# A perceiver layer on one core: pools of their own for keys and ctx weights, the last projection ahead of the experts' blocks, experts' matrices asked for one by one, deeper buffers in the late scan

## The chip, the cores and the metric

The kernel runs on one core of one Trainium2 chip. The metric is the device time of one execution in microseconds (us); lower is better. The kernel before took 1546.52 us in the median of three runs (1540.41 to 1550.73). All data are fp32.

The names of the engines in the profile: PE is TensorE (matmuls; PEld is its loading of weights), DVE is VectorE, ACT is ScalarE, POOL is GpSimd, SP is SyncE, which here only issues transfers (DMAs). Each engine works through its own list of instructions in order; an instruction that has to wait holds everything behind it on its engine.

## The reference, cut to what matters

Four batches of 256 tokens of width 256 go through one layer of three parts, each added to the residual stream x:

```python
x = x + cross_attention(layernorm(x), ctx)      # 8 heads of 64; keys and values of
                                                # 256 own + 4096 ctx positions
# mixture of depths: a small router sorts each batch's tokens
xn      = layernorm(x)
s       = gelu(xn @ r_w1 + r_b1) @ r_w2
top 64 tokens of a batch    -> self-attention of 16 heads
the other 192, in order     -> ssm: conv, silu, h = dA * h + dBu, y = sum(h * C), gate
x = x + scattered back
# mixture of experts, 8 experts, 2 per token
top_w, top_i = top_k(softmax(x @ router_w.T), 2)
h = silu(x @ gate[e]) * (x @ up[e]);  y = h @ down[e]
x = x + sum over the two experts of top_w * y
```

## The kernel before, in words

**The attention's loop** (L1205 to 1634) has 128 steps n, each one eighth of a group G of two heads of one batch, and two more to run out. A step makes scores (L1374), takes the maximum and the exponentials, turns them on DVE (`pt`, L1438) and multiplies them with the values (`po`, L1447). In between it makes the next group's keys (`k_chunk` L1321, `k_self`) and values (`v_chunk` L1351) from ctx chunks. Weights of the group, the batch's turned input `x1T` and the keys `kt` all come from the pool `wk`, together with the work tiles of scores and exponentials. When the last group of a batch is through, `finish_batch` (L1504) multiplies the heads' outputs with the output weights (`project`, L1492) and adds the product to x (`add`, L1500). For the last batch most of that product stands inside the loop's last step; what is left, the last pair of heads of the second half, is queued as a background task.

**Background tasks.** Other parts of the layer are written as generators: `routed(b)` (L892) is the router, the self-attention of the top tokens, the ssm with its scan, and the way back for batch b; `sortable` and `dispatch` (L1039) choose experts for the tokens of tiles 0 to 5 and sort them into blocks of one expert each. A planner places them in the program: `slot(budget)` (L1168) goes through the list of active tasks and runs a task on by one `yield` if its due time has come and its stated cost fits the budget; `now` is moved on by an estimate of the work in front. So the order of the instructions on every engine is fixed when the program is built; there is no scheduler beside it. Three batches' tasks fit beside the attention. The last batch's (b = 3) need the attention's end and run beside the experts' blocks; they use `ssm_scan_late` (L777).

**The late scan.** 16 steps i. ACT makes the decays `dal` (four exponentials of 128x191, L805) one step ahead into one of two tiles `das`; DVE multiplies (L838), scans (L839), multiplies by C (L845) and adds halves (L846) in a tile `db` of three buffers; PE adds up the rest (`yps`, L813). After the scan the gate (`zs`, L866), two products on PE (`pssd` L871, `psback` L881) and an addition bring the batch back to x; then `prepare` (L1792) makes the input of the dense experts.

**The blocks** (`ordered`, L1680). 19 blocks (NB) of 128 sorted tokens. For each block j: three loads of 512 KB, gateT, upT and downT, of the block's expert, whose number SP reads from a tile (L1686); a gather of 128 rows (`xg`, POOL, L1700); a turn on PE and a copy on ACT (`psxb`, `xTb`, L1712, L1715); `half(j, 0)` and `half(j, 1)`, 16 matmuls each into `p0b` and `p1b` (L1721), which come from one pool of three PSUM tiles; `gated` (L1668): a tanh on ACT, two operations on DVE; and, one block later, `down(j - 1)`: eight matmuls into `pdb` (L1735), a copy on ACT (`yb`, L1742) and the write of 128 rows to memory (`ysd`, L1743). The loads and the write are all issued by SP: blocks 0 to 2 are loaded ahead, and `load(j + 2)` comes at the end of block j, behind the write of block j - 1. The experts' tiles come from the pool `fw` with three buffers for each of the three names; this pool is opened after those of the attention are closed, so its tiles lie where theirs lay, and a first load waits for the last reader there.

**The end.** `collect` (L1769) gathers for each token its two rows of `ysd` and adds them. Tiles 6 and 7 (256 tokens) go through all 8 experts densely (`experts`, L1837): for each expert gate, up and down products. Experts 0 and 1 are loaded by `load(NB)` and `load(NB + 1)` in `ordered`, the next always one ahead.

Of the kernel before, what the change touches and what calls it, by code (L numbers as in the profile page):

```python
# [8 lines left out]
F32 = mybir.dt.float32  # L9
# [5 lines left out]
P = 128  # L15
# [3 lines left out]
KD = D // P  # L19
# [27 lines left out]
def perceiver_layer(ctx: ExitStack, tc: tile.TileContext, a: dict, out: bass.AP):  # L47
# [729 lines left out]
    def ssm_scan_late(b, st):  # L777

        SG = 4
        K = DS // SG
        pool = late["pool"]
        delta = st["delta"]
        spread = {}

        das = [pool.tile([P, SG, NBOT], F32, name=f"dal{i}") for i in range(2)]
        for t in das:
            nc.gpsimd.memset(t[:, :, 0:1], 0.0)

        def load(k):
            if k < K:
                for o, name in enumerate(("bbl", "cbl")):
                    t = spread[k, o] = pool.tile([P, SG, NBOT], F32, tag=name, name=name, bufs=2)
                    nc.scalar.dma_start(
                        out=t,
                        in_=st["bcd"][o, SG * k : SG * (k + 1), :].partition_broadcast(P),
                    )


        def decay(i):
            k, m = divmod(i, NDT)
            if k < K:
                for s in range(SG):
                    nc.scalar.activation(  # L805
                        das[i % 2][:, s, 1:], delta[:, m, 1:], AF.Exp,
                        scale=cs["amat"][:, m, SG * k + s : SG * k + s + 1],
                    )
# [12 lines left out]

        yps = st["yps"] = late["psum"].tile([P, 2, 512], F32, name="yps")
        zero = pool.tile([P, SG, NBOT], F32, tag="dbl", name="zero", bufs=3)[:, :2]
        nc.gpsimd.memset(zero, 0.0)
        for i in range(2):
            nc.tensor.matmul(
                yps[:, i, : 2 * NBOT], ident, zero.rearrange("p s t -> p (s t)"),
                start=True, stop=False,
            )
        yield 0.0, 0  # L830
        decay(0)
        yield 0.0, 3.8
        u = st["u"]
        for i in range(K * NDT):
            k, m = divmod(i, NDT)
            decay(i + 1)
            db = dbl[i] = pool.tile([P, SG, NBOT], F32, tag="dbl", name="db", bufs=3)
            nc.vector.tensor_tensor(db, spread[k, 0], bc(u[:, m, :], 1, SG), ALU.mult)  # L838
            nc.vector.tensor_tensor_scan(  # L839
                out=db.rearrange("p s t -> p (s t)"),  # L840
                data0=das[i % 2].rearrange("p s t -> p (s t)"),
                data1=db.rearrange("p s t -> p (s t)"),
                initial=0.0, op0=ALU.mult, op1=ALU.add,
            )
# [358 lines left out]
    NG = B * NHP  # L1203
    NJ = QK // 32
    with ExitStack() as s1:  # L1205
        ctp = s1.enter_context(tc.tile_pool(name="xctx", bufs=4))
        wk = s1.enter_context(tc.tile_pool(name="xwk", bufs=2))
        ps_s = s1.enter_context(tc.tile_pool(name="ps_s", bufs=1, space=PSUM))

        def load_weights(G, names, tag, bufs):  # L1210
            hp = G % NHP
            t = wk.tile([P, len(names), KD, P], F32, tag=tag, name=tag, bufs=bufs)
            for i, name in enumerate(names):
                nc.sync.dma_start(
                    out=t[:, i],
                    in_=a[name].rearrange("(c p) m -> p c m", p=P)[:, :, hp * P : (hp + 1) * P],
                )
            return t
# [68 lines left out]
            yield  # L1287

        def turn_x(b):
            x1Ts[b] = wk.tile([P, KD, T], F32, tag="x1T", name="x1T", bufs=1)  # L1290
            ps = bank("psx1")
            for c in range(KD):
                for h in range(2):
                    nc.tensor.transpose(
                        ps[:, c * T + h * P : c * T + (h + 1) * P],
                        x1s[b][:, h, c * P : (c + 1) * P], ident,
                    )
            nc.scalar.copy(x1Ts[b].rearrange("p c t -> p (c t)"), ps)
# [22 lines left out]
        def k_chunk(G, g):  # L1321
            b = G // NHP
            if G not in kts:
                kts[G] = wk.tile([P, 4, QK], F32, tag="kt", name="kt")
            ct = load_ctx(b, g)
            ps = ps_m.tile([P, 512], F32, tag="m", name="psk")
            for c in range(KD):
                nc.tensor.matmul(  # L1328
                    ps, wqk[G][:, 0, c, :], ct[:, c, :],
                    start=(c == 0), stop=(c == KD - 1),  # L1330
                )
            keys_out(G, g * (CK // 4), ps)

        def k_self(G):
            x1T = x1Ts[G // NHP]
            if G not in kts:
                kts[G] = wk.tile([P, 4, QK], F32, tag="kt", name="kt")
            ps = ps_m.tile([P, 512], F32, tag="m", name="psks")
            for i in range(2):
                for c in range(KD):  # L1340
# [178 lines left out]
        with tc.manual_schedule():  # L1519
# [14 lines left out]
            for n in range(N + 2):  # L1534
# [61 lines left out]
                else:  # L1596
# [25 lines left out]
                        turn(n - 1, 1)  # L1622
                    if last:
                        normalize(m)
                        if m % 8 == 7:
                            start_first(finish_batch(m // 8))
                b = n // 32 + 1
                if b < B:
# [14 lines left out]
    with ExitStack() as s4, tc.manual_schedule():  # L1643
# [7 lines left out]

        late["pool"] = s4.enter_context(tc.tile_pool(name="late", bufs=1))

        def load_expert(e):
            ts = []
            for name, n, m in (("gateT", KD, HID), ("upT", KD, HID), ("downT", NHC, D)):
                t = fw.tile([P, n, m], F32, tag=name, name=name)
                view = a[name].rearrange("e (c p) m -> p e c m", p=P)
                if isinstance(e, int):
                    nc.sync.dma_start(out=t, in_=view[:, e])  # L1660
                else:
                    nc.sync.dma_start(
                        out=bc(t, 1, 1), in_=view[:, bass.ds(e, 1)]
                    )
                ts.append(t)
            return ts

        def gated(pg, pu, out, n):  # L1668

# [9 lines left out]

        def ordered():  # L1680

            weights = {}

            def load(j):
                if j < NB:
                    e = nc.values_load(  # L1686
                        order["experts"][0:1, j : j + 1], engines=[mybir.EngineType.SP],
                        min_val=0, max_val=E - 1,
                    )
                    weights[j] = load_expert(e)  # L1690
                else:
                    first[j - NB] = load_expert(j - NB)

            ys = dram.tile([NB * P, D], F32, name="ysd", bufs=1)
            xgs, xTs, hs = {}, {}, {}
# [34 lines left out]
            def down(j):  # L1730
# [9 lines left out]
                        yield 0.86  # L1740
                y = fk.tile([P, D], F32, name="yb")
                nc.scalar.copy(y, ps[:, :D])  # L1742
                nc.sync.dma_start(out=ys[j * P : (j + 1) * P, :], in_=y)  # L1743
                yield 0.86

            for j in range(3):
                load(j)
            for j in range(4):
                gather(j)
            turn_block(0)  # L1750
            for j in range(NB):
                pg = yield from half(j, 0)
                pu = yield from half(j, 1)
                turn_block(j + 1)
                gather(j + 4)
                rest = down(j - 1)
                yield next(rest, 0.9)

                hs[j] = fk.tile([P, NHC, P], F32, name="hb")
                gated(pg, pu, hs[j].rearrange("p m i -> p (m i)"), 512)  # L1760
                yield from rest
                if j:
                    load(j + 2)
            yield 0.9
            yield from down(NB - 1)

            start(collect(NSORT, ys, order["slots"], order["weights"]))

# [68 lines left out]
        def experts():  # L1837
# [1 line left out]
            weights = dict(first)  # L1839
            x4T = dense["x4T"]  # L1840
            for e in range(E):
                if 0 < e < E - 1:
                    weights[e + 1] = load_expert(e + 1)
                wg_, wu_, wd_ = weights[e]
                hT = fp.tile([P, NHC, nt * P], F32, tag="hTl", name="hTe", bufs=2)
                for n0 in range(0, nt * P, 512):
# [31 lines left out]
        while "ready" not in order:  # L1878
            now[0] += 1.0
            slot(5.0)  # L1880
        late["prepare"] = prepare
        for took in ordered():
            now[0] += took
            slot(5.0)
# [51 lines left out]
```

## Time and profile before

| | |
|---|---|
| median of three runs | 1546.52 us (1540.41 to 1550.73) |
| profiled execution | 1548.97 us, its span 1547.3 us |
| mean clock granted to TensorE | 0.979 |
| PE busy | 1458.9 us (94%) |
| DVE busy | 1059.8 us (68%) |
| ACT busy | 757.8 us (49%) |
| POOL busy | 410.6 us (27%) |
| transfers | 223.41 MB, 144 GB/s over the span |
| gateT, upT, downT: issue to landing, median | 4.6, 5.6, 6.5 us (27 each, 512 KB) |

The profile is one execution; its span runs from the first to the last instruction, and the execution's own time is 1.7 us more. A row of a table of waits names the engine, its line and the tile that waits, behind the arrow who ended the wait, and then us in total, the number of waits and the longest. In the chain of waits, the work that ended last is followed back, at each step to what released it. In a timeline the bracket holds the idle time before the instruction and what ended it. In the table by stage, each row is a stretch of the span with the busy us of every engine (and instructions), the clock granted to PE as a share of full speed, the mean busy share of the 16 DMA engines, and what they moved.

### The profile page before, as it was taken

Reading aid. Unit: us, or ns where it says so; the run is one execution under the profiler, and the core shown is the slowest. Engines: PE = TensorE matmul, PEld = TensorE weight load, DVE = VectorE, ACT = ScalarE, POOL = GpSimd, SP = SyncE. Lnnn points to the kernel's source line nnn. Section 1 sums busy time; section 2 is a strip of 40 time slices with the busy share of each in tenths; the row PEclk is TensorE's granted clock in tenths of the full one; section 3 lists DMA queues with packets and bytes.
Section 4 is the critical chain, followed back from the end, with each engine's and each line's share of the span. In section 5 each row is a group of like instructions: output and inputs, shape, how many; then the busy total and the mean of one; then the engine's idle time right before and its main releaser. Section 6 shows DMA issues by size and latency. Waiting matters only on the chain.

```text
span 1547.3 us, 37278 instructions
## 1 busy us (share of the span) xinstructions
PE 1458.9 (94%) x15686; PEld 1039.8 (67%) x15686; DVE 1059.8 (68%) x1825; ACT 757.8 (49%) x1485; POOL 410.6 (27%) x464
## 2 busy tenths in 40 slices
PE   7999999999999999999999999999998968889799
PEld 3757667576666576775766666758575658778687
DVE  1666666666599976565899866757999554589553
ACT  3444454455566745454666453656654413544211
POOL 1000000000079950000599600003998010110100
PEclk9999999999999999999999999999999979999999
DMA  7455433514245434333554434244452206678471
GB/s 233 135 155 161 157 126 125 174 63 155 95 145 168 161 109 153 119 102 111 162 164 131 144 127 150 68 156 133 141 171 91 74 27 213 208 258 270 157 231 48
DMA packets 157768, 223.41 MB, mean 144 GB/s; under 512 B 14977, under 2 KB 76161, under 8 KB 157601
## 3 DMA queue, kind: packets, MB, share of 16 engines
q1 hardware_dynamic: 152368, 211.45, 42.1%
q10 hardware_dynamic: 3744, 5.51, 1.2%
q0 software_dynamic: 1488, 4.07, 0.9%
q8 instruction: 124, 2.03, 0.5%
q14 instruction: 44, 0.35, 0.1%
HBM read 216.56 MB, written 4.42 MB: 143 GB/s over the span
## 4 chain that ended last, share of the span: by engine, by line
PE 64%; POOL 15%; DVE 10%; DMA 4%; issue 4%; ACT 2%; SPq 0%; ACTq 0%; DVEq 0%; POOLq 0%
PE po L1447 12%; PE su L1381 11%; PE psv L1365 11%; PE psk L1328 9%; POOL y L751 5%; POOL db L736 5%; POOL db L749 5%; DVE sp L1401 3%; PE su L1389 2%; PE pg L1853 2%; PE pu L1853 2%; PE pde L1866 2%; PE p1b L1721 2%; DMA gateT<-in_gateT 2%; DVE db L743 1%
## 5 line engine op out<-in xcount | busy, mean ns | idle before, releaser
L1401 DVE TENSOR_SCALAR_CACHE_REDUCE sp<-su 128x1088 f32<-128x1088 f32 x256 | 318.8, 1281 | 182.0 <-PE su L1389 181.8
L1438 DVE STREAM_TRANSPOSE pt<-sp 128x1088 f32<-128x1088 f32 x256 | 328.0, 1295 | 58.7 <-PE po L1447 58.7
L1429 ACT ACTIVATE sp<-sp,nb 128x1088 f32<-128x1088 f32 x256 | 305.2, 1195 | 13.5 <-DVE nb L1418 13.3
L1447 PE MATMUL po<-pt,v 128*64 128x128 f32 x4352 | 262.9, 278 | 2.3 <-DVE pt L1438 1.3
L1381 PE MATMUL su<-kt,qz 64*32 64x512 f32 x4096 | 256.3, 609 | 4.4 <-DVE nb L1418 3.7
L1328 PE MATMUL psk<-ctx,wk 128*128 128x512 f32 x512 | 244.3, 611 | 10.5 <-DMA ctx<-in_ctxT 7.4
L1365 PE MATMUL psv<-wv,ctx 128*128 128x128 f32 x2048 | 250.8, 279 | 0.2 <-ACT da L731 0.2
L1447 PEld LDWEIGHTS po<-pt,v 128*64 128x64 f32 x4352 | 240.9, 139 | 13.9 <-issue 7.5
L1365 PEld LDWEIGHTS psv<-wv,ctx 128*128 128x128 f32 x2048 | 236.6, 192 | 6.4 <-issue 1.3
L1328 PEld LDWEIGHTS psk<-ctx,wk 128*128 128x128 f32 x512 | 91.3, 191 | 94.8 <-issue 84.4
L1316 ACT COPY kt<-psk 128x512 f32<-128x512 f32 x128 | 74.6, 584 | 158.2 <-PE psk L1328 157.9
L1381 PEld LDWEIGHTS su<-kt,qz 64*32 64x32 f32 x4096 | 63.4, 108 | 123.8 <-issue 94.6
L751 POOL TENSOR_TENSOR y<-y,db 128x192 f32<-128x192 f32 x192 | 135.2, 704 | 15.0
L1369 ACT COPY v<-psv 128x512 f32<-128x512 f32 x144 | 79.1, 557 | 120.0 <-PE psv L1365 118.7
L743 DVE TENSOR_TENSOR_SCAN db<-da,db 128x384 f32<-128x384 f32 x96 | 122.5, 1276 | 14.4 <-POOL db L736 3.7
L395 POOL TENSOR_TENSOR kbd<-qk,hmask 128x512 f32<-128x512 f32 x8 | 8.2, 1042 | 413.2 <-ACT qk L385 413.2
L749 POOL TENSOR_TENSOR db<-db,cb 128x384 f32<-128x384 f32 x96 | 111.1, 1157 | 24.3 <-DVE da L741 24.3
L736 POOL TENSOR_TENSOR db<-bb,xc 128x384 f32<-128x384 f32 x96 | 110.9, 1176 | 0.2
L1389 PEld LDWEIGHTS su<-kt,qz 128*32 128x32 f32 x2048 | 34.6, 109 | 109.4 <-issue 109.4
L731 ACT ACTIVATE da<-delta,A_log_sb 128x192 f32<-128x192 f32 x192 | 75.6, 447 | 51.9 <-DVE da L741 39.0
L1484 ACT COPY ao<-po 128x128 f32<-128x128 f32 x32 | 8.4, 263 | 150.6 <-PE po L1447 150.6
L1413 PEld LDWEIGHTS su<-mq,same 128*128 128x128 f32 x256 | 41.3, 193 | 54.7 <-DVE mq L1408 37.9
(298 smaller groups left out, 1589.5 us busy)
## 6 DMA issues: line engine op xcount, KB each, us to landing
ctx<-in_ctxT SPq DMA_DIRECT2D x256, 512.0 KB, 4.8
gateT<-in_gateT SPq DMA_DIRECT2D x27, 512.0 KB, 4.6
upT<-in_upT SPq DMA_DIRECT2D x27, 512.0 KB, 5.6
downT<-in_downT SPq DMA_DIRECT2D x27, 512.0 KB, 6.5
bb<-bcd SPq DMA_DIRECT2D x24, 192.0 KB, 4.3
cb<-bcd SPq DMA_DIRECT2D x24, 192.0 KB, 3.6
wv<-in_wv SPq DMA_DIRECT2D x32, 128.0 KB, 2.3
in_w<-in_in_w SPq DMA_DIRECT2D x32, 128.0 KB, 3.7
```

Of the source, the lines that this page charges most:

```text
L736: nc.gpsimd.tensor_tensor(db, bbs[k], bc(xc[:, m, :], 1, SG), ALU.mult)
L743: nc.vector.tensor_tensor_scan(out=db, data0=da, data1=db, initial=0.0, op0=ALU.mult, op1=ALU.add,)
L749: nc.gpsimd.tensor_tensor(db, db, cbs[k], ALU.mult)
L751: nc.gpsimd.tensor_tensor(y[:, m, :], y[:, m, :], db[:, s, :], ALU.add)
L1328: nc.tensor.matmul(ps, wqk[G][:, 0, c, :], ct[:, c, :], start=(c == 0), stop=(c == KD - 1),)
L1365: nc.tensor.matmul(ps[:, i * P : (i + 1) * P], lhsT, wv[G][:, w, c, :], start=(c == 0), stop=(c == KD - 1),)
L1369: nc.scalar.copy(v.rearrange("p k d -> p (k d)"), ps[:, : n * P])
L1381: nc.tensor.matmul(su[q * 32 : (q + 1) * 32, SC[j] + lo : SC[j] + lo + 512], qT[r, j, s * 32 : (s + 1) * 32], kt[r, q, lo : lo + 512], sta ...
L1401: nc.vector.tensor_scalar(out=sps[n][j], in0=su[:, SU[j] : SU[j] + QK], scalar1=1.0, scalar2=None, op0=ALU.mult, op1=ALU.max, accum_out=nm ...
L1429: nc.scalar.activation(sps[n][j], sps[n][j], AF.Exp, bias=nbs[n][:, j : j + 1], accum_out=lss[b][:, hp, s, j : j + 1],)
L1438: nc.vector.transpose(pts[m, j][:, i, :], sps[n][j])
L1447: nc.tensor.matmul(pos[m][j * HD : (j + 1) * HD, :], vts[m // 2, k // 4][:, k % 4, j * HD : (j + 1) * HD], pts[m, j][:, :, kk * 32 : (kk + ...
```

## The change

- The attention's weights, `x1T` and the keys `kt` move from the pool `wk` to a pool of their own, `wke`, which is opened ahead of `wk`; so tiles of the attention lie at other addresses.
- In the loop's last step, `finish_batch(B - 1)` is run to its end at once, no longer queued; and one more `slot(5.0)` of background tasks stands ahead of the blocks. With it, what is left of the last projection comes before block 0.
- `load` takes a matrix number too: gateT of block j + 3 is asked for after `half(j, 0)`, upT after `half(j, 1)`, downT of block j + 2 after `down(j - 1)`.
- The write of a block's rows is issued by ACT in place of SP.
- The dense experts start with three loaded, and stay two ahead.
- `das` has three tiles in place of two, `db` and `zero` four buffers in place of three.

The diff, without the changes of one name in `turn_x`, `k_chunk` and `k_self` (`wk` to `wke`) and the buffer numbers in `ssm_scan_late`:

```diff
         delta = st["delta"]
         spread = {}
 
-        das = [pool.tile([P, SG, NBOT], F32, name=f"dal{i}") for i in range(2)]
+        das = [pool.tile([P, SG, NBOT], F32, name=f"dal{i}") for i in range(3)]
         for t in das:
             nc.gpsimd.memset(t[:, :, 0:1], 0.0)
 
...
     NG = B * NHP
     NJ = QK // 32
     with ExitStack() as s1:
+
         ctp = s1.enter_context(tc.tile_pool(name="xctx", bufs=4))
+        wke = s1.enter_context(tc.tile_pool(name="xwe", bufs=2))
         wk = s1.enter_context(tc.tile_pool(name="xwk", bufs=2))
         ps_s = s1.enter_context(tc.tile_pool(name="ps_s", bufs=1, space=PSUM))
 
         def load_weights(G, names, tag, bufs):
             hp = G % NHP
-            t = wk.tile([P, len(names), KD, P], F32, tag=tag, name=tag, bufs=bufs)
+            t = wke.tile([P, len(names), KD, P], F32, tag=tag, name=tag, bufs=bufs)
             for i, name in enumerate(names):
                 nc.sync.dma_start(
                     out=t[:, i],
...
                         turn(n - 1, 1)
                     if last:
                         normalize(m)
-                        if m % 8 == 7:
+                        if n == N + 1:
+                            for _ in finish_batch(B - 1):
+                                pass
+                        elif m % 8 == 7:
                             start_first(finish_batch(m // 8))
                 b = n // 32 + 1
                 if b < B:
...
 
         late["pool"] = s4.enter_context(tc.tile_pool(name="late", bufs=1))
 
+        parts = (("gateT", KD, HID), ("upT", KD, HID), ("downT", NHC, D))
+
+        def load_part(e, i):
+
+            name, n, m = parts[i]
+            t = fw.tile([P, n, m], F32, tag=name, name=name)
+            view = a[name].rearrange("e (c p) m -> p e c m", p=P)
+            if isinstance(e, int):
+                nc.sync.dma_start(out=t, in_=view[:, e])
+            else:
+                nc.sync.dma_start(out=bc(t, 1, 1), in_=view[:, bass.ds(e, 1)])
+            return t
+
         def load_expert(e):
-            ts = []
-            for name, n, m in (("gateT", KD, HID), ("upT", KD, HID), ("downT", NHC, D)):
-                t = fw.tile([P, n, m], F32, tag=name, name=name)
-                view = a[name].rearrange("e (c p) m -> p e c m", p=P)
-                if isinstance(e, int):
-                    nc.sync.dma_start(out=t, in_=view[:, e])
-                else:
-                    nc.sync.dma_start(
-                        out=bc(t, 1, 1), in_=view[:, bass.ds(e, 1)]
-                    )
-                ts.append(t)
-            return ts
+            return [load_part(e, i) for i in range(3)]
 
         def gated(pg, pu, out, n):
 
...
 
         def ordered():
 
-            weights = {}
-
-            def load(j):
-                if j < NB:
-                    e = nc.values_load(
-                        order["experts"][0:1, j : j + 1], engines=[mybir.EngineType.SP],
-                        min_val=0, max_val=E - 1,
-                    )
-                    weights[j] = load_expert(e)
-                else:
-                    first[j - NB] = load_expert(j - NB)
+            weights, numbers = {}, {}
+
+            def load(j, i):
+
+                if i == 0:
+                    if j < NB:
+                        numbers[j] = nc.values_load(
+                            order["experts"][0:1, j : j + 1],
+                            engines=[mybir.EngineType.SP], min_val=0, max_val=E - 1,
+                        )
+                        weights[j] = []
+                    else:
+                        numbers[j] = j - NB
+                        weights[j] = first[j - NB] = []
+                weights[j].append(load_part(numbers[j], i))
 
             ys = dram.tile([NB * P, D], F32, name="ysd", bufs=1)
             xgs, xTs, hs = {}, {}, {}
...
                         yield 0.86
                 y = fk.tile([P, D], F32, name="yb")
                 nc.scalar.copy(y, ps[:, :D])
-                nc.sync.dma_start(out=ys[j * P : (j + 1) * P, :], in_=y)
+                nc.scalar.dma_start(out=ys[j * P : (j + 1) * P, :], in_=y)
                 yield 0.86
 
             for j in range(3):
-                load(j)
+                for i in range(3):
+                    load(j, i)
             for j in range(4):
                 gather(j)
             turn_block(0)
             for j in range(NB):
                 pg = yield from half(j, 0)
+                load(j + 3, 0)
                 pu = yield from half(j, 1)
+                load(j + 3, 1)
                 turn_block(j + 1)
                 gather(j + 4)
                 rest = down(j - 1)
...
                 gated(pg, pu, hs[j].rearrange("p m i -> p (m i)"), 512)
                 yield from rest
                 if j:
-                    load(j + 2)
+                    load(j + 2, 2)
             yield 0.9
             yield from down(NB - 1)
+            load(NB + 2, 2)
 
             start(collect(NSORT, ys, order["slots"], order["weights"]))
 
...
             weights = dict(first)
             x4T = dense["x4T"]
             for e in range(E):
-                if 0 < e < E - 1:
-                    weights[e + 1] = load_expert(e + 1)
+                if 0 < e < E - 2:
+                    weights[e + 2] = load_expert(e + 2)
                 wg_, wu_, wd_ = weights[e]
                 hT = fp.tile([P, NHC, nt * P], F32, tag="hTl", name="hTe", bufs=2)
                 for n0 in range(0, nt * P, 512):
...
             now[0] += 1.0
             slot(5.0)
         late["prepare"] = prepare
+        now[0] += 1.0
+        slot(5.0)
         for took in ordered():
             now[0] += took
             slot(5.0)
```

More of the change, by code (lines that the diff above doesn't have):

```diff
@@ L805, in decay @@
                     nc.scalar.activation(
-                        das[i % 2][:, s, 1:], delta[:, m, 1:], AF.Exp,
+                        das[i % 3][:, s, 1:], delta[:, m, 1:], AF.Exp,
                         scale=cs["amat"][:, m, SG * k + s : SG * k + s + 1],
@@ L822, in ssm_scan_late @@
         yps = st["yps"] = late["psum"].tile([P, 2, 512], F32, name="yps")
-        zero = pool.tile([P, SG, NBOT], F32, tag="dbl", name="zero", bufs=3)[:, :2]
+        zero = pool.tile([P, SG, NBOT], F32, tag="dbl", name="zero", bufs=4)[:, :2]
         nc.gpsimd.memset(zero, 0.0)
@@ L836, in ssm_scan_late @@
             decay(i + 1)
-            db = dbl[i] = pool.tile([P, SG, NBOT], F32, tag="dbl", name="db", bufs=3)
+            db = dbl[i] = pool.tile([P, SG, NBOT], F32, tag="dbl", name="db", bufs=4)
             nc.vector.tensor_tensor(db, spread[k, 0], bc(u[:, m, :], 1, SG), ALU.mult)
@@ L840, in ssm_scan_late @@
                 out=db.rearrange("p s t -> p (s t)"),
-                data0=das[i % 2].rearrange("p s t -> p (s t)"),
+                data0=das[i % 3].rearrange("p s t -> p (s t)"),
                 data1=db.rearrange("p s t -> p (s t)"),
@@ L1289, in turn_x @@
         def turn_x(b):
-            x1Ts[b] = wk.tile([P, KD, T], F32, tag="x1T", name="x1T", bufs=1)
+            x1Ts[b] = wke.tile([P, KD, T], F32, tag="x1T", name="x1T", bufs=1)
             ps = bank("psx1")
@@ L1323, in k_chunk @@
             if G not in kts:
-                kts[G] = wk.tile([P, 4, QK], F32, tag="kt", name="kt")
+                kts[G] = wke.tile([P, 4, QK], F32, tag="kt", name="kt")
             ct = load_ctx(b, g)
@@ L1336, in k_self @@
             if G not in kts:
-                kts[G] = wk.tile([P, 4, QK], F32, tag="kt", name="kt")
+                kts[G] = wke.tile([P, 4, QK], F32, tag="kt", name="kt")
             ps = ps_m.tile([P, 512], F32, tag="m", name="psks")
```

## The prediction

> **What bounds the kernel now.** I read the page first (TensorE, PE, busy 94% of a span of 1547.3 us, so only its gaps can be won), then its slices: PE's row reads 9 throughout but for the first slice and the 31st to 38th (8, 9, 6, 8, 8, 8, 9, 7), some 1160 to 1470 us, where the cross-attention ends and the blocks of experts run. A table by stage, with stage limits from the timeline (the last scores end at 1246.4, the last values at 1273.6, the late scan starts near 1333, its gate ends at 1442.4, the dense experts start at 1456.4), gives us, PE, PEld, DVE, ACT, POOL busy (x instructions), clock, DMA share, GB/s:
>
> ```profile
> 1246.40:1273.60 27.20, 20.38 (x182) 17.77 (x182) 12.08 (x26) 2.48 (x4) 3.96 (x4) 0.75 0.07 20
> 1273.60:1333.20 59.60, 49.00 (x307) 43.96 (x306) 22.07 (x55) 26.97 (x53) 7.34 (x11) 0.92 0.62 201
> 1333.20:1442.40 109.20, 98.43 (x694) 89.80 (x693) 93.09 (x111) 44.54 (x121) 11.60 (x11) 0.98 0.79 259
> 1442.40:1456.40 14.00, 7.32 (x29) 4.51 (x29) 2.99 (x9) 4.21 (x9) 4.83 (x6) 0.90 0.51 162
> 1456.40:1547.30 90.90, 86.31 (x392) 75.20 (x392) 41.30 (x104) 13.59 (x34) 6.51 (x7) 0.97 0.39 127
> ```
>
> See three things. In the first row the DMA engines do nothing (0.07) and PE is at a 0.75 clock. In rows two and three PE idles 59.6 - 49.0 + 109.2 - 98.4 = 21.4 us; in row three VectorE (DVE) works 93.1 of 109.2: the scan and the blocks' gates together are its bound, not PE. The last row is PE's own.
>
> Who makes PE and DVE wait? The waits of SP's queue over 1236 to 1442 (us in total, times, longest):
>
> ```profile
> SPq L1743 <- ACT yb L1742: 67.6, 10, 16.6
> SPq L1743 <- ACT dal L805: 39.3, 8, 7.8
> SPq L1686 <- DVE part L1093: 32.3, 1, 32.3
> SPq L1662 <- DVE pt L1438: 17.4, 1, 17.4
> SPq L1662 <- PE po L1447: 13.9, 1, 13.9
> ```
>
> SP stands at the write of a block's result (L1743) for 107 us, and the next expert's three loads stand behind it; the last two lines are the first load, waiting for the attention's last transpose and values although the experts' numbers were known. The chain of waits (start, us, what) shows the price:
>
> ```profile
> 1269.97 3.67 PE po L1447 x64
> 1273.65 3.83 DMA gateT<-in_gateT
> 1277.62 3.75 PE p0b L1721 x16
> ...
> 1333.18 7.95 DMA gateT<-in_gateT
> 1341.27 3.54 PE p0b L1721 x16
> ...
> 1352.56 6.79 DMA gateT<-in_gateT
> 1359.49 1.13 PE p0b L1721 x8
> ```
>
> Each time DVE, which needs the block's product for its gate, stands still too; its timeline (start, us, ..., idle before) has the two large ones:
>
> ```profile
> 1350.19 0.69 DVE L1672 SCALAR_TENSOR_TENSOR sg<-sg,p0b 128x512 f32<-128x512 f32 x1 [4.14 <-ACT sg L1671]
> 1367.28 0.69 DVE L1672 SCALAR_TENSOR_TENSOR sg<-sg,p0b 128x512 f32<-128x512 f32 x1 [5.19 <-ACT sg L1671]
> ```
>
> **What the skill says.** "DMA: Bandwidth & Descriptors", Anatomy of one DMA: "DMA engines do not wait on semaphores"; the wait stands on the issuing sequencer. The SP lines agree. The same page, Issuing engines are not separate DMA queues: a transfer moved to another engine saves only issue time. So I count nothing for ACT's queue but the freed SP. "TensorE: Matmul & The Clock Gate", Part 1, What's actually happening: after an idle window of about 3.4 us PE runs at half clock. Agrees: sixteen p0b matmuls took 3.75 and 3.54 us after waits of 3.20 and 3.94 us, 1.95 us warm.
>
> **The change, part by part.** Times below are of the profiled execution, 1548.97 us (span plus 1.7 us), 2.45 us above the median of 1546.52 (1540.41 to 1550.73); I take the difference in span from the median.
>
> 1. *Pools in the attention* (wke). The order of instructions of both kernels is equal on every engine through the attention; only the first load's wait changes, from the last po (1273.6) to the last su (1246.4). So nine loads, 4.7 MB, start 27 us earlier; at the 245 to 280 GB/s of the busier slices that is 17 to 19 us, hidden under the last values. Saves the 3.83 us at 1273.65. Without that cover these 3.8 us return.
>
> 2. *Projection ahead of the blocks.* psx now stands right behind psxb(0): about 1274.4 instead of 1282.87, so the last router chain starts 8.5 us earlier. It issues no transfer of its own, and the nine loads are ahead of it on SP, the gathers ahead on POOL. But on ACT the copy xTb(0) now stands behind the router's rs, so p0b(0) starts near 1277 as before: the gain of 1 is spent here. Behind p0b(0), gate 0 on DVE stands behind the router's ranks, and p1b(1) waits for that gate's buffer: PE stalls some 3.7 us near 1287 (estimate, from the durations of the chain between 1283.58 and 1292.56), and the router's later matmuls are queued behind it. One table load less on ACT (1.28 us each in the trace; the tanh no longer falls between two gelus). Start of the scan: 8.5 - 3.7 + 1.3 = 6.1 us earlier, 1335.85 to 1329.7.
>
> 3. *Loads one by one, results written by ACT.* A matrix is asked for as soon as its buffer is free, two and a half to three blocks ahead (6.8 us each, so at least 17 us, against landings of 4.6 to 11 us), and SP stands behind nothing else. PE's 10.1 us of waits for gateT go, and with them DVE's waits at the gate. DVE's work from the scan's start to its last gate: 16 steps of 0.95 + 1.76 + 0.96 + 0.56 = 4.27 with small gaps, 14 gates of 0.69 + 0.69 = 1.39, 3.8 for the attention and the rest: 91.6, plus 12.2 idle: 103.8. After: one gate fewer, since the scan starts a block earlier against the blocks: 90.2, plus 1.5 idle that I leave: 91.7. Saved 12.1. ACT gets 19 issues of 0.32 to 0.48 us, 6 to 9 us at 41% busy: hidden while DVE is the bound. The 1.83 MB per block (weights, gather, write) over 7.1 us are 258 GB/s, beside 280 at a share of 0.85 in the busiest slices: not bound, but close.
>
> 4. *Three da, four db.* ACT's dal may run three ahead; DVE showed 1 us of waits for it. One small memset more on POOL, which is 11% busy. Counted at nothing; if ACT is delayed by 3, this is what covers it.
>
> 5. *What is late next.* A write on ACT waits for the lane of an earlier transfer, and xTb, tanh and dal stand behind it. In the order, 17 of the 19 stand on lanes whose transfer is two blocks old; two do not (blocks 3 and 6, behind fresh gateT and downT loads): from nothing to 3 + 4 us, I take 2.5 on the path. At the end, gate 18 and the last pdb now follow the scan: 1.39 + 0.9, 2.3 us more. The last write then lands later (6.7 us in the trace), and the first gathered row, needed on DVE ahead of the dense gates, may come 0 to 4 us late; I take 0. The dense experts, with two prefetched, need 10.36 us of PE each against 6.5 us to land: no change. The 7.5 us between psback and pg stay.
>
> Sum: 6.1 + 12.1 - 2.5 - 2.3 = 13.4 us off the span, 1547.3 to 1533.9; on the median's scale 1533.1, say 1533 us (0.9%).
>
> **Rivals.** *A: the loads covered other idleness.* DVE loses its waits for gateT but then waits for PE or ACT, since all three share 16 scan steps and 19 blocks: of the 12.1 us only a third is kept. For it: the seven idle gates of row three add to 12.2 us and only two are large, 9.3 us together; ACT's dal held PE's weight loads for 7.5 us. Against: PE has 98 us of work in 109. Gives 6.1 + 4 - 4.8 = 5.3: 1541 us. *B: the coupling goes wholly.* No lane wait, the p1b(1) stall hidden behind router matmuls (3.7 back), no idle on DVE: 13.4 + 2.5 + 3.7 = 19.6, less PE's own limit (141 us of work and 5 cold from 1274 still ends well before DVE): 1527 us. For it: PE's clock excess of 6.4 us in these stages goes with the waits. *C, the slower side: ACT becomes the queue that SP was.* Place: the write on ACT. If it waits for a fresh weight load each block (SP's writes waited for loads three times, up to 2.3 us), 19 times w are lost on the path of tanh and gate. From w = 0.7 us nothing is won; from 1.5 us it is slower by over 1%; at 1.6 us: 19 x 1.6 - 13.4 = +17, 1564 us. For it: ACT is one queue for tanh, dal and copies. Against: the age of the lanes. *D: it does nothing*, because the transfers themselves are the bound once they are bunched (row three at 0.79): 1546 us. Against: the pace of 6.8 us per block was held where no load was late.
>
> **How the numbers follow.** Forecast 0.40 (its own range 1529 to 1538), A 0.20, B 0.25, C 0.10, D 0.05. One per cent, about what a measurement of this kernel can tell from no change (three runs spread over 0.67%), is 15.5 us: faster below 1531.1. That is B and a quarter of the forecast, 0.35; slower above 1562 is half of C, 0.05; the rest 0.60. The range 1523 to 1546 leaves out C, most of D and B's end.
>
> **What would show it.** In the profile after: first gateT issued near 1246.5; p0b(0) near 1277 with a warm clock; psx near 1274; a PE stall of 3 to 4 us at p1b(1); the scan's first step near 1329.7 (step 2); no wait of PE for gateT and no DVE gap over 2 us in the scan (step 3); psback's end near 1435 instead of 1448.9; 90.9 us for the dense experts. Wrong if ACT stands at its writes for more than 5 us in sum on the path, if the scan starts later than 1333, or if the last write's lateness stalls the dense gates.

## The result, and the profile after

| | before | after |
|---|---|---|
| median of ten runs | 1549.38 us (1540.41 to 1552.11) | 1536.55 us (1532.57 to 1539.69) |
| ratio, 95% interval | | 0.9928 (0.9914 to 0.9942) |
| span of the profiled execution | 1547.3 us | 1532.4 us |
| clock granted to PE | 0.979 | 0.984 |

The kernel became 12.8 us faster by the medians. The spans of the two profiles differ by 14.9 us, which is not the same thing: single executions lie up to 7 us apart in after and 12 us in before.

The table by stage of after (same columns as in the prediction; the stages end at the last scores, the last values, the first step of the late scan, its gate, and the first dense matmul):

```profile
1245.00:1272.30 27.30, 20.41 (x185) 17.79 (x182) 12.70 (x28) 2.48 (x4) 5.14 (x6) 0.75 0.57 193
1272.30:1327.50 55.20, 48.88 (x330) 44.12 (x328) 24.06 (x60) 27.32 (x56) 6.95 (x11) 0.97 0.57 167
1327.50:1427.30 99.80, 92.09 (x663) 84.97 (x663) 90.73 (x102) 43.38 (x115) 11.59 (x11) 0.98 0.86 278
1427.30:1441.90 14.60, 9.02 (x40) 6.01 (x38) 3.36 (x9) 4.81 (x10) 1.55 (x2) 1.00 0.41 131
1441.90:1532.40 90.50, 85.96 (x392) 74.84 (x392) 42.09 (x106) 13.61 (x34) 9.82 (x11) 0.97 0.36 116
```

The prediction drew the line between its second and third row at 1333.2; the first step of the scan stands at 1335.85. The two rows of before with the line there:

```profile
1273.60:1335.80 62.20, 51.60 (x324) 46.53 (x323) 24.53 (x62) 29.19 (x60) 7.34 (x11) 0.92 0.62 203
1335.80:1442.40 106.60, 95.83 (x677) 87.22 (x675) 90.63 (x103) 42.32 (x115) 11.60 (x11) 0.98 0.79 259
```

The first row's DMA share went from 0.07 to 0.57: the nine loads now lie under the last values. In the third row DVE does the same work (90.6 and 90.7 us) in 7 us less time, while the DMA engines reach 0.86 and 278 GB/s. PE is the busier of the two in this row, before and after (92.1 beside 90.7 of 99.8 us), so it is not DVE's stage alone, as the prediction took it to be.

The waits of SP's queue and of PE, two views of after over 1236 to 1442 and 1273 to 1442 (us in total, times, longest):

```profile
SPq L1669 <- PE p0b L1732: 51.0, 16, 25.4
...
SPq L1669 <- PE pdb L1746: 28.9, 15, 2.9
SPq L1669 <- PE p1b L1732: 17.6, 6, 5.4
```

```profile
PE p1b L1732 <- DVE sg L1679: 7.2, 5, 3.5
PE psx L1824 <- ACT x4l L211: 3.6, 2, 3.4
PE yps L813 <- DVE db L846: 3.4, 1, 3.4
PE p0b L1732 <- ACT xTb L1726: 3.1, 3, 2.0
```

SP still stands, but where it should: at buffers that PE has not yet given back. The loads of gateT go out 17 to 44 us ahead of their use (4 to 18 before), and no wait of PE for a load is left. Two waits are new or longer: the first line (2.3 us before), of which 3.5 us are one stall at block 1, and the 3.4 us in which PE waits for DVE's first scan step. (The wait of psx belongs to the way to the dense experts; in before it is 5.4 us.) PE's timeline (start, us, ..., idle before) shows the stall and the start of block 0:

```profile
1275.67 2.05 PE L1732 MATMUL p0b<-xTb,gateT 128*128 128x128 f32 x16 [1.96 <-ACT xTb L1726]
...
1287.13 2.51 PE L1732 MATMUL p1b<-xTb,upT 128*128 128x128 f32 x16 [3.53 <-DVE sg L1679]
```

Since the attention, which the change leaves as it was, ends between 1270.0 and 1275.3 us in the profiles of this study, the runs are compared from its end on. Each column is us, read from the timelines: from the end of the last po to the scan's first step; from there to the end of zs; to the start of the addition of psback; to the first dense matmul; to the end. (zs is the scan's gate, psback the product that takes the batch back to x, pg the first product of the dense experts.)

| profiled run | to scan | scan to zs | to psback's addition | to pg | to end | sum |
|---|---|---|---|---|---|---|
| before | 62.2 | 106.5 | 6.6 | 7.4 | 90.9 | 273.7 |
| after | 55.2 | 99.7 | 9.5 | 5.1 | 90.5 | 260.1 |
| before, pools | 57.5 | 103.8 | 6.6 | 7.3 | 91.3 | 266.4 |
| before, projection | 56.6 | 99.7 | 9.5 | 5.1 | 91.9 | 262.8 |
| before, write on ACT | 62.9 | 98.9 | 6.6 | 5.1 | 90.4 | 263.8 |
| before, loads and write | 62.2 | 98.9 | 6.6 | 6.1 | 90.4 | 264.1 |
| after, projection queued | 57.7 | 102.1 | 6.6 | 6.2 | 91.0 | 263.6 |
| after, one pool | 56.3 | 99.7 | 9.5 | 5.1 | 91.9 | 262.4 |
| after, write on SP | 55.2 | 99.3 | 9.5 | 5.4 | 90.7 | 260.2 |
| after, two da, three db | 56.8 | 99.8 | 9.5 | 5.1 | 90.5 | 261.7 |
| after, down product held back | 58.9 | 99.8 | 6.8 | 7.3 | 90.8 | 263.5 |
| after, product held back, copy later | 55.2 | 99.7 | 6.8 | 5.1 | 90.4 | 257.2 |
| after, psn earlier | 52.1 | 103.5 | 9.4 | 7.3 | 91.1 | 263.4 |
| after, both of these | 53.6 | 105.2 | 9.4 | 5.1 | 90.6 | 263.8 |

Each row is one execution. That of the pools took 5.4 us less than the median of its runs, that of the write on ACT 4.4 us less; the others lie within 3 us of theirs. So the rows say where the time goes; what a part is worth is read from the medians and ratios.

Between the two profiles nearly the whole gain is before the dense experts: 7.0 us to the scan's start, 6.8 in the scan, 2.4 between psback and pg, against 3.0 lost at the scan's end; 0.4 at the end and 1.3 us of the attention's own scatter make up the 14.9.

### The profile page after: what moved, and what is told of

It reads as the page before. It is cut to its first block, busy times and chain, and to the rows that moved or that the text cites. A ratio compares the mean times of both kernels' runs of the same rounds, so it can differ in the third digit from the quotient of the medians.

```text
span 1532.4 us, 37303 instructions
## 1 busy us (share of the span) xinstructions
PE 1452.4 (95%) x15686; PEld 1034.5 (68%) x15686; DVE 1062.5 (69%) x1825; ACT 758.1 (49%) x1484; POOL 411.9 (27%) x465
## 4 chain that ended last, share of the span: by engine, by line
PE 65%; POOL 15%; DVE 11%; issue 4%; ACT 2%; DMA 1%; SPq 0%; ACTq 0%; DVEq 0%; POOLq 0%
PE po L1449 12%; PE su L1383 11%; PE psv L1367 11%; PE psk L1330 9%; POOL y L751 6%; POOL db L736 5%; POOL db L749 5%; DVE sp L1403 3%; PE su L1391 2%; PE pg L1868 2%; PE pu L1868 2%; PE pde L1881 2%; PE p1b L1732 2%; DVE db L743 1%; DVE pt L1440 1%
## 5 line engine op out<-in xcount | busy, mean ns | idle before, releaser
L1431 ACT ACTIVATE sp<-sp,nb 128x1088 f32<-128x1088 f32 x256 | 305.1, 1195 | 13.4 <-DVE nb L1420 13.2
```

The lines of the kernel that those rows point to most:

```text
L1431: nc.scalar.activation(sps[n][j], sps[n][j], AF.Exp, bias=nbs[n][:, j : j + 1], accum_out=lss[b][:, hp, s, j : j + 1],)
```

## The experiments

**One part at a time, from before.** Theory 1 was the prediction's: SP's queue of loads holds PE and through it DVE. Theory 2: only the projection's place counts. "Us less" below is worked out from the ratio, with the time of before measured beside each run (medians of 1547.5 to 1548.0 us).

The pools alone (`wke` as in the diff):

> Before with the pools alone. Theory 1 (what holds PE and DVE is SP's queue of loads): the nine first loads start near 1245, block 0's first matmuls follow the turn at once with a warm clock, 4 us earlier; the last projection behind them too, so the scan starts some 4 us earlier; the waits at later loads stay. 4 us less, 1545. Theory 2 (only the place of the projection counts, and loads are hidden by other idleness): the 4 us are lost at the next wait, 0 to 1 us less.

Measured: 1543.67 us, ratio 0.9977 (0.9966 to 0.9988), 3.6 us less. Block 0 begins 1.3 us after the attention, and its sixteen matmuls take 2.05 us (warm); in before it begins after 4.0 us, and they take 3.75 us (cold). As theory 1 said.

The projection alone:

```diff
-                        if m % 8 == 7:
+                        if n == N + 1:
+                            for _ in finish_batch(B - 1):
+                                pass
+                        elif m % 8 == 7:
...
         late["prepare"] = prepare
+        now[0] += 1.0
+        slot(5.0)
```

> Before with the last projection ahead of the blocks alone. Theory 1: block 0 still begins near 1277.6, cold; the router chain starts 8 us earlier and the scan some 6 us, but the waits for gateT stay: 5 us less, 1544. Theory 2: the whole gain is here, 11 to 13 us less.

Measured: 1539.54 us, ratio 0.995 (0.9931 to 0.9969), 7.7 us less: between the two. The reason is not in either theory. SP's waits over 1270 to 1445 of this run:

```profile
SPq L1746 <- ACT yb L1745: 67.1, 11, 15.1
SPq L1746 <- ACT dal L805: 38.8, 8, 9.3
```

and PE's over 1273 to 1442:

```profile
PE p1b L1724 <- DVE sg L1675: 6.6, 4, 3.3
...
PE p0b L1724 <- DMA gateT<-in_gateT: 2.6, 1, 2.6
```

SP stands behind the writes for the same 106 us as before, the loads of gateT go out only 4.4 to 10.9 us ahead of use after the first three experts, and still none is late but block 0's own. In before the two that held PE longest in the scan had gone out 8.1 and 6.9 us ahead, and landing took 7.9 and 6.8 us. The loads of the same two blocks differ here. The first goes out in both runs 5.7 us behind the first of four broadcasts (`bbl`, `cbl`, 384 KB each) and 0.4 us ahead of `out_w`, so beside the same transfers, but 9.9 us ahead of its use. The second goes out only 4.7 us ahead and has landed by then; it stands 3.7 us behind the load of `awv`, in before 1.3 us behind it. So the first has more lead, and the second lands sooner. That `awv` made the second slow in before is read from the times of issue; no run moves it alone.

The write on ACT alone:

```diff
-                nc.sync.dma_start(out=ys[j * P : (j + 1) * P, :], in_=y)
+                nc.scalar.dma_start(out=ys[j * P : (j + 1) * P, :], in_=y)
```

> Before with the results written by ACT in place of SP, alone; loads are still asked for in threes. Theory 1: the loads no longer stand behind yb; they go out about two blocks (13 us) ahead of use, which is longer than they take to land (4.6 to 11), so the waits of p0b for gateT and the two large waits of DVE (9.3 us) go: 8 us less, 1541. If it is the asking one by one that matters, less than half of that. Theory 2: 0 to 2 us less.

Measured: 1540.31 us, ratio 0.9962 (0.9944 to 0.9981), 5.9 us less. The waits of DVE at the gates within the scan fall from 12.2 to 4.0 us; loads of gateT, still asked for in threes, go out 11 to 26 us ahead, block 0's apart, and PE waits for none of them in the scan.

Loads one by one and the write on ACT (no pools, no projection, no buffers):

> Before with loads one by one, two dense experts ahead, and results written by ACT; no other part. Theory 1: 9 us less, 1540, at most 1 to 2 better than the write alone. Theory 2: 0 to 3 us less.

Measured: 1540.15 us, ratio 0.9954 (0.9936 to 0.9972), 7.1 us less, with the same scan (98.9) as the write alone. The asking one by one shows nothing of its own; the intervals overlap.

The three gains are 3.6, 7.7 and 7.1 us, 18.4 in sum; all together give 0.9928 or 11.1 us. They overlap: two of them remove the same waits. That led to a new theory, "overlap", tested by taking one part away.

**One part away, from after.**

The projection queued again (the diff of the projection above, reversed):

> After, with the last projection queued as before; all other parts kept. Overlap (pools, projection and loads each remove the same waits of PE for gateT, so one of them more or less costs little): the scan starts 57 us after the attention's end as with the pools alone, in place of 55, takes 99 us, but gate and product of the last block are then ahead of the scan's end, so the stretch from zs to the addition of psback is 6.6 in place of 9.5 us: between 1 us more and 2 us less than after, 1535 to 1538. Each part on its own (as predicted, the projection brings its 6 us whatever the loads do): 5 to 6 us more than after, 1542.

Measured: 1535.46 us, ratio 0.9921 (0.9905 to 0.9938); after itself 0.9928. Without the projection nothing is lost that can be measured. But the scan took 102.1 us, not 99: with every load in time DVE still waited 7.9 us at the gates. The two views, DVE's waits over the scan in this run and in after:

```profile
DVE sg L1676 <- ACT sg L1675: 7.9, 6, 3.5
```

```profile
DVE sg L1679 <- ACT sg L1678: 3.3, 4, 1.7
```

So a part of the gates' idle time remains with every load in time; it depends on how scan and blocks lie against each other. That is the mechanism of rival A.

One pool again:

```diff
-        wke = s1.enter_context(tc.tile_pool(name="xwe", bufs=2))
...
-                kts[G] = wke.tile([P, 4, QK], F32, tag="kt", name="kt")
+                kts[G] = wk.tile([P, 4, QK], F32, tag="kt", name="kt")
```

> After, with the attention's weights and keys back in one pool with the work tiles. Overlap: the first load goes out at the attention's end again, p0b of block 0 runs cold, scan start 56.6 in place of 55.2 us after the attention's end: 1 to 2 us more, 1538. Each part on its own: the 3.8 us of the first load return, 1540.

Measured: 1538.93 us, ratio 0.9944 (0.9926 to 0.9962): some 2.5 us more, between the 1 to 2 us of overlap and the 3.8 us of the other theory; the intervals of this run and of after overlap, so the times don't decide. The scan starts 1.1 us later, as overlap had it, but block 0's matmuls were not cold (2.02 us after a wait of 3.07 us).

Beside the run with the projection alone this one says more, since it is the projection plus loads, write and buffers. Stage by stage the two are alike (56.3 and 56.6 us to the scan, 99.7 in it, 9.5 and 5.1 behind it, in both), and so are the ratios, 0.9944 and 0.995. Once the projection is ahead, loads, write and buffers together add nothing that these runs can measure.

The write on SP again:

```diff
-                nc.scalar.dma_start(out=ys[j * P : (j + 1) * P, :], in_=y)
+                nc.sync.dma_start(out=ys[j * P : (j + 1) * P, :], in_=y)
```

> After, with the results written by SP again, loads one by one. Overlap: the loads stand behind the writes, SP stands there for some 100 us, but with the projection ahead no load comes later than its use, as in the run with the projection alone: 0 to 1 us more, 1537. Each part on its own: the waits of p0b for gateT come back, 5 to 10 us more, 1543.

Measured: 1535.38 us, ratio 0.9924 (0.9902 to 0.9946): nothing. With loads one by one the writes may stay on SP: SP stands some 60 us at them (not 100), and the loads of gateT go out 17 to 44 us ahead there too.

The scan's buffers as before:

```diff
-        das = [pool.tile([P, SG, NBOT], F32, name=f"dal{i}") for i in range(3)]
+        das = [pool.tile([P, SG, NBOT], F32, name=f"dal{i}") for i in range(2)]
...
-            db = dbl[i] = pool.tile([P, SG, NBOT], F32, tag="dbl", name="db", bufs=4)
+            db = dbl[i] = pool.tile([P, SG, NBOT], F32, tag="dbl", name="db", bufs=3)
```

> After, with two da and three db again. As predicted (counted at nothing): ACT's dal are ahead of the scan with two as with three, DVE waits for dal under 1 us in sum: within 1 us of after. Rival: with writes on ACT the third buffer is what covers ACT's delays: the scan's stretch grows from 99.7 by 2 to 4 us.

Measured: 1537.94 us, ratio 0.9932 (0.9911 to 0.9952), and the scan's stretch 99.8 us: the buffers do nothing here.

**The scan's end and its start.** The last block's gate and down product lie between zs and psback in after, and cost 3 us. First, the product held back:

```diff
-            yield 0.9
+            while B - 1 not in done:
+                yield 0.5
             yield from down(NB - 1)
```

> After, with the last block's down product held back until batch 3 has gone through psback. If those eight matmuls and the gate they wait for are what lengthened the way from zs to the addition of psback (9.5 against 6.5 us), it falls back to 6.6: 2.5 to 3 us less than after, 1534, since pdb then fits into PE's 3.4 us wait for x4l. Rival: what stretches it is ACT's wait at its write ahead of dsort (3.36 us in the profile after), which stays: 0 to 0.5 us less; or the last write comes 3 us later and the dense gates wait for its rows: no less.

Measured: 1537.46 us, ratio 0.9934 (0.9918 to 0.995): no gain. The stretch to psback's addition did fall to 6.8 us, but the next one rose from 5.1 to 7.3. ACT's timeline shows whom it met:

```profile
1438.14 0.37 ACT L1753 COPY yb<-pdb 128x256 f32<-128x256 f32 x1 [3.38 <-PE pdb L1746]
...
1438.90 1.28 ACT L194 ACT_TABLE_LOAD   x1 [0.39 <-ACT yb L1753]
1440.19 0.30 ACT L194 ACTIVATE rs<-mv,eps_t 128x2 f32<-128x2 f32 x1
```

The block's copy waits for the product that was moved, and the table load that batch 3's normalization needs stands behind it. Neither rival named this. Part of the time was also lost early, at a cold start of block 0 (last section): the scan started 58.9 us after the attention in this execution. (ACT's 3.36 us "wait at its write" ahead of dsort was no limit: it reads as a wait of 1.35 us for pssd here.) So, with that edit kept, the copy was moved too (in `down`):

```diff
+                while j == NB - 1 and "x4T" not in dense:
+                    yield 0.5
                 y = fk.tile([P, D], F32, name="yb")
```

> After, with the last block's down product behind psback, as in the run that held it back, and its copy and write on ACT behind x4Tl, so that ACT's table load and rs no longer wait for it (2.2 us there). From zs to the addition 6.7 us, from there to pg 5.1: 2.8 us less than after, 1534. Rival: the last write is later by some 5 us and something waits for its rows (dense gates on DVE): no less.

Measured: 1533.78 us, ratio 0.9914 (0.9896 to 0.9932), the lowest of all. The profile has 6.8 and 5.1 us as expected, 2.8 less; the times agree, but the interval reaches that of after, so the stages show it and the medians only suggest it. In ACT's timeline the table load no longer waits:

```profile
1433.35 1.28 ACT L194 ACT_TABLE_LOAD   x1
1436.92 0.30 ACT L194 ACTIVATE rs<-mv,eps_t 128x2 f32<-128x2 f32 x1 [2.28 <-DVE mv L184]
```

Second, the router's next step made due earlier:

```diff
-        yield (4.5 if late else 1.0), 1.4
+        yield (1.0 if late else 1.0), 1.4

         ps = bank("psn")
```

> After, with the due time of the router's next step at 1.0 in place of 4.5, which puts psn ahead of p1b of block 1 and what follows (low, pos, perm, psg) ahead of gate 1 and of block 2. If the path to the scan is what was late (psn stood 6 us behind the ranks on PE, low 6 us behind its use on DVE), the scan starts 4 to 5 us earlier, 51 us after the attention's end; one more half block then lies behind the scan, so the way from zs to psback's addition grows by up to 2 us: 3 us less than after, 1533.5. Rival: PE is the bound by now, and all of it returns as a longer scan stretch or end: 0.

Measured: 1536.38 us, ratio 0.9934 (0.9915 to 0.9953): none. The scan does start 3.1 us earlier, and then takes 103.5 in place of 99.7 us. PE's timeline has the place:

```profile
1330.43 3.79 PE L1732 MATMUL p0b<-xTb,gateT 128*128 128x128 f32 x16 [6.63 <-ACT xTb L1726]
```

PE stands 6.6 us, runs cold, and DVE waits at the next two gates (3.40 and 3.33 us). The copy xTb is late because ACT stood; ACT's timeline:

```profile
1328.20 0.39 ACTq L479 DMA_DIRECT2D out_w<-in_out_w  x1
1328.64 1.49 ACT L805 ACTIVATE dal<-delta,A_log_sb 128x191 f32<-128x191 f32 x4 [6.33 <-DMA downT<-in_downT]
1330.03 0.35 ACT L1726 COPY xTb<-psxb 128x256 f32<-128x256 f32 x1
```

ACT's queue stood 5.9 us at the issue of the load `out_w`, until a load of downT had landed, and dal, xTb and the tanh behind it stood too. In after the same issue waited 0.3 us. This is rival C's mechanism, ACT as the queue that SP was, at a load in place of a write. So the result is the rival's, but by a stall and not because PE was full, and the run doesn't show what an earlier start is worth without the stall. Why that issue waits for downT is not shown.

> Both of the last two edits. If they are worth what each shows and do not meet: 5 us less than after, 1531.5. If the half block that the earlier scan leaves over fills the end: as the first of them alone, 3 us less.

Measured: 1536.15 us, ratio 0.9918 (0.9895 to 0.994): no better than the product held back with its copy later. ACT stands 6.9 us at the issue of `out_w` here too, and with the scan earlier against the blocks the product of the last block but one also lies between pssd and psback, which the edit leaves there: 9.4 us from zs to the addition, where that edit alone had 6.8.

## Why the prediction was right, step by step

The forecast was 13.4 us less; measured were 12.8 by the medians (14.9 between the profiles). The terms, against the two profiles:

- *Step 1, pools.* Right. First load at 1245.1 (1246.5 predicted), block 0 at 1275.7 (1277), warm at 2.05 us: the gain is spent at xTb, as stated. Alone it was worth 3.6 us.
- *Step 2, start of the scan*, 6.1 predicted: 7.0 from the attention's end. The stall at p1b(1), 3.7 predicted, was 3.5. Right.
- *Step 3*, 12.1 predicted from the scan's start to the last block's gate within it: 8.2 measured (104.2 to 96.1 us), and 6.8 up to zs. This is the term that was mis-sized. The gates' waits went from 12.2 to 3.3 (8.9 of the 10.7 taken), and one gate fewer (1.4) came as stated. Against that stand 1.4 us in the first step, where DVE ran beside POOL (below), a wait for psas (0.57), and, between the last gate and zs, a wait for yps (1.65 us, 0.31 before). The prediction left DVE 1.5 us of idle time as if it alone bounded the stage.
- *Step 3's cause* was only half right. Late loads did make the two large waits, and mending SP's queue removes them (run with the write alone). But moving the projection removes them as well, with SP as blocked as ever; and with all loads in time 7.9 us of idle gates can remain. That the loads stand behind the write was true, and not by itself the cost.
- *The lanes of step 5* (a write, it says, waits for the earlier transfer on its lane), 2.5 predicted: nothing. In after each of the 19 writes on ACT left 0.03 us behind its copy.
- *Step 4* at nothing: right.
- *The end in step 5*, 2.3 us more: 3.0, by the mechanism named. With the product held back 2.7 of them went, the gate still behind the scan.
- "The 7.5 us between psback and pg stay": wrong by 2.4 us in the kernel's favour. In before, DVE's queue had a gathered row ahead of the normalization; DVE's timeline of before and then of after:

```profile
1452.81 0.48 DVE L1784 SCALAR_TENSOR_TENSOR x_sb<-yg,eweights,x_sb 128x256 f32<-128x256 f32 x1 [1.97 <-DMA yg<-ysd,slots]
1453.21 0.16 DVE L201 RECIPROCAL rs<-rs 128x2 f32<-128x2 f32 x1
```

```profile
1439.24 0.16 DVE L203 SCALAR_TENSOR_TENSOR nmr<-mv,rs 128x2 f32<-128x2 f32 x1
1442.76 0.48 DVE L1799 SCALAR_TENSOR_TENSOR x_sb<-yg,eweights,x_sb 128x256 f32<-128x256 f32 x1 [3.35 <-DMA yg<-ysd,slots]
```

The 1.97 us of waiting and the 0.48 us of the addition stood ahead of the reciprocal; after, the row comes behind it, and its 3.35 us fall where PE has dense products to go on with. The prediction had that wait only as a risk.

The sum was right in part by luck. Up to zs the scan gained 5.3 us less than the 12.1 predicted; the 2.5 us taken off for ACT's lanes, which cost nothing, and the 2.4 us behind psback, which it did not have, almost fill that gap (0.9 too little at the start, 0.7 at the end and 0.4 in the dense experts are the rest). Nor did the parts count one by one, as the sum has it. Rival A's mechanism exists, with a smaller price than I gave it; B's full release was not reached, nor was it by either run that started the scan earlier; C's price was not paid at the writes in any run (at most 0.52 us between copy and write), but its mechanism came in at a load, in the two runs with the router's step earlier; D is excluded by the gain itself, and the DMA engines moved 278 GB/s at a share of 0.86 with no late load.

What stays open: whether the transfers beside the late loads of before made them late; what the router's earlier step is worth if ACT does not stand at `out_w`; and which alignment of scan and blocks is best. The planner's costs decide that, and only single points of it were tried. After with loads in threes and writes on SP, all else kept, was not run.

## What to carry to other kernels

When several edits each remove the same wait, their single gains do not add (18.4 us in sum, 11 together). From the finished kernel the projection's move or ACT's write can be taken back with no loss that was measured, and the pools for some 2.5 us; price an edit by taking it away from the finished kernel too. A long wait on a queue that only issues transfers is no cost in itself: what counts is whether the transfer lands before its use. On a queue that also computes it is one, for all that stands behind it (5.9 us at one issue on ACT). When work is moved out of the way at a stage's end, look at the queue of every engine it uses: the product left PE's path, but its copy held ACT's table load, and only moving both gained.

## What the runs showed of the hardware that was not expected

- *DVE and POOL slow each other in two operations.* In after's first scan step DVE's multiplication took 1.61 us and the addition 1.28, beside 0.96 and 0.56 in the following steps, while POOL made its two kbd. The timelines of DVE and of POOL:

```profile
1330.42 1.61 DVE L845 TENSOR_TENSOR db<-db,cbl 128x768 f32<-128x768 f32 x1
1332.07 1.28 DVE L846 TENSOR_TENSOR db<-db 128x384 f32<-128x384 f32 x1
```

```profile
1329.99 2.95 POOL L395 TENSOR_TENSOR kbd<-qk,hmask 128x512 f32<-128x512 f32 x2 [2.20 <-ACT qk L385]
```

  In before the same two kbd took 2.04 us, while DVE mostly stood idle ahead of a gate. No run was made to isolate this, but the traces sort themselves. In six of the fourteen (after among them) the kbd fall on these two operations, which take 1.61 to 1.62 and 1.28 us, and the second kbd 1.75 or 1.76. In two (write on ACT; loads and write) the kbd meet the addition, which takes 1.35 us. In the other six they meet neither, each kbd takes 1.04 us, and the two operations take 0.96 and 0.56.
- *PE's speed after the same gap is not always the same.* The prediction read half speed after waits of 3.20 and 3.94 us. After a wait of 1.96 us, block 0's sixteen matmuls took 2.05 us in after and 3.79 us in the run with the down product held back, whose instructions up to there are the same:

```profile
1274.31 3.79 PE L1732 MATMUL p0b<-xTb,gateT 128*128 128x128 f32 x16 [1.96 <-ACT xTb L1726]
```

  The same sixteen took 3.53 and 3.21 us after 1.96 us in two more runs (psn earlier with the end edits; two da, three db), and 2.02 us after 3.07 us in the run with one pool. In the three slow cases the scan started 3.7, 1.5 and 1.6 us later after the attention than in their counterparts (after, psn earlier, after). So 1.5 to 3.7 us of the scatter between executions can lie here, and a profile alone cannot tell edits of this size apart.
